# Two of four row tiles turned by TensorE, new plan costs for DMA turns, and seven block products for eight at the end of a fused quantised layer

## The chip, the cores and the metric

The kernel runs on one core of one Trainium2 chip, as one launch. The metric is the device time of that launch in microseconds (us). The profiler also gives one profiled execution, with a span from its first to its last instruction. A smaller time is better.

TensorE (PE) multiplies into PSUM, VectorE (DVE), ScalarE (ACT) and GpSimd (POOL) work elementwise, and SyncE (SP) issues most transfers. A DMA turn is a transfer that transposes 128-row blocks on its way within SBUF.

## What is computed

`x` is two batches of 1024 rows by 2048, `ctx` two matrices of 2048 x 2048, `weight` one matrix of 2048 x 2048, all f32.

```python
def fake_quant(x, scale, zp):
    q = jnp.clip(jnp.round(x / s + z), 0, 255)
    return (q - z) * s

# first product
x = x + tanh(g_xattn) * (fake_quant(layernorm(x)) @ fake_quant(ctx))
# second product: rows to int8 by their own largest value, weights to -1, 0, 1
h = layernorm(x)
s = 127 / clip(max(abs(h), axis=-1), 1e-5)
xq = clip(round(h * s), -128, 127) / s
scale_w = 1 / clip(mean(abs(weight)), 1e-5)
tw = clip(round(weight * scale_w), -1, 1)
x = x + tanh(g_ffn) * (einsum('bsi,oi->bso', xq, tw) / scale_w)
```

Each second product is therefore 1024 x 2048 x 2048 per batch, with rows that are whole numbers and weights that are -1, 0 or 1.

## The kernel before

**Tiles.** The rows are 16 tiles of 128; tiles 0 to 7 are batch 0, tiles 8 to 15 batch 1. In each batch they are taken in the order 6, 7, 0, 1, 2, 3, 4, 5 (`last_first`, L970; `rows` for batch 1, L1052). A tile's rows stay in `resid` as f32 from load (L351) to store (L829).

**First product.** `norm1` (L371) takes a tile's statistics (L378), quantises it to int16 on ScalarE (L434) and clips it to f16 on VectorE (L437). The tile is then turned, so that its columns lie on partitions: in batch 0 by PE with 128x128 transposes into PSUM (L444) and two evictions (L450), in batch 1 by one DMA turn on SP's queue (L454). Row sums come from GpSimd additions in batch 0 (L460 to L465) and from ScalarE in batch 1 (L473). `context` (L526) loads blocks of the context (L541), quantises them on ScalarE (L547), clips them on VectorE (L550) and adds them for a column term (L557, `column_term` L574). All of them come to rest in `ca`, in two halves h of 1024 columns. `first(t, h)` (L602) is 16 steps of two f16 matmuls with 512 columns (L611), and an addition to the rows (L620). `terms` (L635) adds the row and column terms (L640).

**Second product.** `norm2` (L660) takes one or two tiles: squares with their sum on ScalarE (L677), largest value on VectorE (L684), small operations on one number per row (L690 to L709). `norm2_tile` (L736) quantises to int16 on ScalarE (L748), casts to f16 on VectorE (L757) and turns the tile: by PE (L762) with two evictions (L768), of which the first `by_act` go to ScalarE and the rest to VectorE, or by a DMA turn (L774). `second(t, h, ...)` (L801) is 16 matmuls for each 512 columns: 8 pairs of blocks, f16 rows stationary, fp8 weights moving (L814), then an addition with the row's scale (L823) and a store (L829), by SP for two tiles of batch 1 and by GpSimd for all others.

**Weights.** They are loaded twice in part (L854), summed (L865), quantised (L899), clipped to fp8 (L903) and turned in units of two bytes: output blocks 0 to 5 by PE (L909, L913), 6 to 15 by DMA turns (L917). They rest in `tw`, four units q of 512 columns. Until then `tw` and `ca` also serve as landing places.

**What sets the order.** Nothing is issued where it stands in the code. Each `step(engine, weight, due, do, rd, wr, take, give, dma, hold, port)` only books a piece of work: its engine, its planned time, a due time, its keys read and written, and a buffer that it takes from a pool (`work`: 4, `tp` for turned rows: 5, `mm`: 3 PSUM tiles, `tr`: 2). `dma` is the planned time of a transfer on the shared DMA engines, and `port` marks work that VectorE and GpSimd may only do one at a time in the plan. `Plan.order` (L62) simulates the engines with these costs, always issuing the step that can begin first, and of several the one that is due first. `Plan.latest` (L123) works new due times back from the end. `give_out` (L153) does both ten times, keeps the shortest plan and issues its steps in that order. So a changed cost of one step may move instructions on any engine.

For a DMA turn, the plan has the queue's own share as the weight and the transfer as `dma`, and SP is held in the plan until earlier transfers are through (L108 and L109):

```python
if dma:
    if port is None:
        end = free[engine] = max(end, dma_free)
    dma_free = max(dma_free, end) + dma
```

**Stages.** Batch 0's first products with h=0, then with h=1, with `norm2` of tiles 6 and 7 as soon as these are done, then of 0 and 1 (L975). The second product of tiles 6, 7, 0 and 1 goes unit by unit along with the arrival of the turned weights (L1005 to L1021), with 128-column matmuls for unit 0. Then tiles 2 to 5. In batch 1 (L1067 to L1092) tiles are planned in pairs, and the planner is free to place second products of the first tiles before first products of the last ones.

Of the kernel before, what the change touches and what calls it, by code (L numbers as in the profile page):

```python
# [9 lines left out]
F32 = mybir.dt.float32  # L10
# [13 lines left out]
class Plan:  # L24
# [128 lines left out]
    def give_out(self):  # L153
        steps = self.steps
        waits = [len(s[4]) for s in steps]
        follow = [[] for _ in steps]
        for n, s in enumerate(steps):
            for m in s[4]:
                follow[m].append(n)
        due, best = [s[2] for s in steps], None  # L160
        for i in range(self.ROUNDS):
            order, ends, passed = self.order(due, follow, waits)
            if best is None or max(ends) < best[0]:
                best = (max(ends), order)
            due = self.latest(ends, passed, follow)
        for n, slot in best[1]:
            if slot is None:
                steps[n][3]()
            else:
                steps[n][3](slot)  # L170
# [3 lines left out]
def flamingo_gated_kernel(  # L174
# [117 lines left out]
    plan = Plan({"work": NWORK, "tp": NTP, "mm": 3, "tr": 2})  # L292
    step = plan.step
    aT, qT, pm = {}, {}, {}
    taken = {}

    def scalars():

        s = {}

        def spread(slot):
            s["pp"] = tr[slot]
            nc.tensor.matmul(s["pp"][:, 2:6], ones32[0:1, :], par1[:, 2:6], start=True, stop=True)
            nc.tensor.matmul(s["pp"][:, 0:2], ones32[0:1, :], tg1, start=True, stop=True)

        def of(i, rs, zc):
            nc.vector.reciprocal(rs, par[:, i : i + 1])  # L310
            nc.vector.tensor_scalar(zc, par[:, i + 1 : i + 2], CENTER, None, ALU.subtract)

        def rest():
            nc.vector.scalar_tensor_tensor(g1, par[:, 2:3], par[:, 4:5], tg[:, 0:1], ALU.mult, ALU.mult)
            nc.vector.scalar_tensor_tensor(g1d1, zc1, -1.0, g1, ALU.mult, ALU.mult)
            nc.vector.scalar_tensor_tensor(g1d2, zc2, -1.0, g1, ALU.mult, ALU.mult)
            nc.vector.tensor_scalar(kd2, zc2, -float(K), None, ALU.mult)
            nc.vector.tensor_scalar(gkd, kd2, g1d1, None, ALU.mult)

        step("ACT", 0.3, 0.0, lambda: nc.scalar.activation(tg1, par1[:, 0:2], AF.Tanh), wr=[("tg1",)], hold=4.0)  # L320
        by = step("PE", 0.6, 6.0, spread, rd=[("tg1",)], wr=[("pp",)], take="tr", hold=6.8)
        step(
            "DVE", 0.2, 6.0, lambda: nc.vector.tensor_copy(par, s["pp"][:, 0:6]), rd=[("pp",)],
            wr=[("par",)], give=[by],
        )
        step("DVE", 0.3, 6.1, lambda: of(2, rs1, zc1), rd=[("par",)], wr=[("p1",)])
        step("DVE", 0.3, 6.2, lambda: of(4, rs2, zc2), rd=[("par",)], wr=[("p2",)])
        step("DVE", 0.9, 10.0, rest, rd=[("p1",), ("p2",)], wr=[("g",)])

    def res(t):  # L330
        return resid[:, t % MT, :]

    def xk(t, h=None):
        return [("x", t % MT, i) for i in ((0, 1) if h is None else (h,))]

    strip = const.tile([P, 30 * 2 * MT], F32, name="strip")
    stats6 = const.tile([P, 4, K // 512, nc.vector.BN_STATS_DIM], F32, name="stats6")
    used = [0]

    def tiny(n=1):  # L340
        used[0] += n
        return strip[:, used[0] - n : used[0]]


    def load_x(t, due, queue, halves=1, hold=0.0):
        w = K // halves
        for h in range(halves):

            def bring(h=h):
                q = nc.sync if queue == "SP" else nc.gpsimd  # L350
                q.dma_start(out=res(t)[:, ts(h, w)], in_=xrow[t][:, ts(h, w)])  # L351

            keys = xk(t) if halves == 1 else xk(t, h)
            step(queue, 0.5, due, bring, wr=keys, dma=2.55 / halves, hold=hold)

    def newton(v, sd):

        n = v.shape[1]
        r, f = tiny(n), tiny(n)
        nc.vector.reciprocal(r, sd)  # L360
        if n == 1:
            nc.vector.tensor_scalar(f, v, r, r, ALU.mult, ALU.mult)
            nc.vector.tensor_scalar(f, f, -0.5, 1.5, ALU.mult, ALU.add)
            nc.vector.tensor_scalar(r, r, f, None, ALU.mult)
        else:
            nc.vector.scalar_tensor_tensor(f, r, -0.5, r, ALU.mult, ALU.mult)
            nc.vector.tensor_mul(f, f, v)
            nc.vector.scalar_tensor_tensor(r, f, 1.5, r, ALU.add, ALU.mult)
        return r

    def norm1(group, dues, by_pe, fold_it, place=None, pieces=1, on_dve=False):  # L371

        n = len(group)
        s = {"mv": tiny(2 * n)}
        key = lambda *a: ("n1", group[0]) + a

        def stats(t, c):
            nc.vector.bn_stats(stats6[:, t % 4, c, :], res(t)[:, ts(c, 512)])  # L378

        def aggr(j, t):  # L380
            nc.vector.bn_aggr(s["mv"][:, ts(j, 2)], stats6[:, t % 4].rearrange("p c s -> p (c s)"))

        def root():
            s["sd"] = tiny(n)
            nc.scalar.activation(s["sd"], s["ve"], AF.Sqrt)

        def var():
            mv = s["mv"].rearrange("p (n s) -> p s n", s=2)
            s["mean"], s["ve"] = mv[:, 0, :], tiny(n)
            nc.vector.tensor_scalar(s["ve"], mv[:, 1, :], LN_EPS, None, ALU.add)  # L390

        def scale():
            r = newton(s["ve"], s["sd"])
            sc, bi = s["sc"], s["bi"] = tiny(n), tiny(n)
            nc.vector.tensor_scalar(sc, r, rs1, None, ALU.mult)
            if n == 1:
                nc.vector.tensor_scalar(bi, s["mean"], sc, -1.0, ALU.mult, ALU.mult)
            else:
                nc.vector.scalar_tensor_tensor(bi, s["mean"], -1.0, sc, ALU.mult, ALU.mult)
            nc.vector.tensor_scalar(bi, bi, zc1, None, ALU.add)  # L400

        for j, t in enumerate(group):
            for c in range(4):
                step(
                    "DVE", 0.69, dues[j], (lambda t, c: lambda: stats(t, c))(t, c), rd=xk(t, c // 2),
                    wr=[("st", t % 4)],
                )
            step(
                "DVE", 0.3, dues[j], (lambda j, t: lambda: aggr(j, t))(j, t), rd=[("st", t % 4)],
                wr=[key("mv")],  # L410
            )
        due = dues[-1]
        step("DVE", 0.16, due, var, rd=[key("mv")], wr=[key("ve")])
        step("ACT", 0.2, due, root, rd=[key("ve")], wr=[key("sd")])
# [4 lines left out]

    def norm1_tile(t, due, by_pe, fold_it, place, pieces, ready, scales, on_dve):  # L420

        s = {}
        key = lambda *a: ("n1t", t) + a
        n = K // pieces

# [699 lines left out]
```

## Time and profile before

| what | us |
|---|---|
| runs, median of 3 | 498.71 (497.04, 498.71, 499.32) |
| profiled execution, its own time | 496.74 |
| its span | 495.0 |
| PE busy | 467.6 |
| VectorE busy | 340.6 |
| ScalarE busy | 276.6 |
| GpSimd busy | 63.5 |
| mean granted clock of TensorE | 0.995 |

1.74 us of the profiled execution lie outside its span. Five groups of instructions, by line and shape, with count, busy time and mean:

| group | count | busy us | mean ns |
|---|---|---|---|
| L611 matmuls 128x512, f16 | 1024 | 230.8 | 379 to 384 |
| L814 matmuls 128x512, fp8 weights | 976 | 214.8 | 379 to 381 |
| L814 matmuls 128x128, fp8 weights | 192 | 11.5 | 219 |
| L762 transposes 128x128 (rows of the second product) | 32 | 2.3 | 219 |
| L774 DMA turns of such rows | 14 | - | - |

The mean time of a matmul is from its start to the end of its own passage; matmuls overlap, so start to start they are closer. The profile names engines as above; "PEld" is PE's load of stationary data, "SPq" SP's queue. A row of 40 digits shows the span in 40 slices of 12.4 us, each digit being the busy share in tenths; the row "PEclk" is the clock that TensorE was granted. In a list of waits, the columns are the total of the waits, their number and the longest. In a timeline, the columns are start, length, engine, line and operation, with the idle time ahead and what ended it in brackets.

### The profile page before, as it was taken

To read this page: it belongs to the slowest core of one execution; us is meant where nothing else is said; L and a number is where in the kernel's file an instruction comes from. 1 tells how busy PE (TensorE), PEld (TensorE's weight loads), DVE (VectorE), ACT (ScalarE), POOL (GpSimd) and SP (SyncE) were. 2 spreads that over 40 slices of the span, in tenths; PEclk is the share of its full clock that TensorE was granted. 3 is DMA by queue.
4 is the path that set the end of the run, shared out by engine and by line. 5 is a ranking of instruction groups with operands and counts; after the bars stand their busy time and mean duration, and the time that the engine had idled before them with its cause. 6 is when DMAs were issued, how large, how long until landed. Compare 5 with 4: busy or idle time off the path is not lost.

```text
span 495.0 us, 6179 instructions
## 1 busy us (share of the span) xinstructions
PE 467.6 (94%) x2422; PEld 223.0 (45%) x2422; DVE 340.6 (69%) x568; ACT 276.6 (56%) x258; POOL 63.5 (13%) x76
## 2 busy tenths in 40 slices
PE   0599999999998799999999999999999999999996
PEld 0244454444467344444444444444444444444442
DVE  4999989959999688556697957632989831572122
ACT  4997896878999988631488364530454430050000
POOL 0574529100000020100100100000000000000000
PEclk9999999999999899999999999999999999999999
DMA  8999968992189999999999995610041542215122
GB/s 293 425 419 424 366 214 338 428 407 81 60 215 366 260 301 295 306 258 330 402 363 341 297 269 189 100 28 1 0 66 47 144 111 102 86 61 153 79 92 85
DMA packets 76170, 108.94 MB, mean 220 GB/s; under 512 B 58220, under 2 KB 58220, under 8 KB 70892
## 3 DMA queue, kind: packets, MB, share of 16 engines
q1 hardware_dynamic: 72064, 93.86, 60.1%
q0 software_dynamic: 4064, 14.68, 7.7%
q8 instruction: 19, 0.31, 0.2%
q14 instruction: 11, 0.09, 0.1%
q10 hardware_dynamic: 12, 0.00, 0.0%
HBM read 77.59 MB, written 16.78 MB: 191 GB/s over the span
## 4 chain that ended last, share of the span: by engine, by line
PE 76%; DVE 14%; DMA 6%; issue 2%; ACT 1%; DVEq 0%
PE mm L814 40%; PE mm L611 32%; DVE resid L640 3%; DMA resid<-in_x_dram 2%; PE tr L814 2%; DVE strip L684 2%; DMA tw<-in_ctx_dram 2%; DVE resid L620 2%; DMA tw<-ca 2%; DVE stats L378 1%; DVE ca L550 1%; DVE ca L903 1%; ACT ca L547 1%; PE tr L444 1%; DVE colg L557 1%
## 5 line engine op out<-in xcount | busy, mean ns | idle before, releaser
L814 PE MATMUL mm<-tw,turned 128*128 128x512 fp8e4 (+1 forms) x1104 | 211.9, 353 | 4.7 <-DMA turned<-work 2.4
L611 PE MATMUL mm<-ca,turned 128*128 128x512 f16 x832 | 187.7, 384 | 0.5 <-DVE ca L550 0.3
L814 PEld LDWEIGHTS <-turned 128*128 128x128 f16 x1168 | 106.8, 98 | 122.7 <-issue 6.3
L611 PEld LDWEIGHTS <-turned 128*128 128x128 f16 x832 | 81.8, 99 | 99.0 <-issue 4.8
L823 DVE SCALAR_TENSOR_TENSOR resid<-mm,am,resid 128x1024 f32<-128x1024 f32 (+1 forms) x31 | 38.6, 1246 | 64.3 <-PE mm L814 64.2
L547 ACT ACTIVATE ca<-ca,scal 128x2048 int16<-128x2048 f32 (+1 forms) x30 | 50.5, 1692 | 36.9 <-DMA ca<-in_ctx_dram 36.4
L677 ACT ACTIVATE work<-resid,strip 128x1024 f32<-128x1024 f32 x32 | 36.4, 1138 | 57.8 <-DVE strip L668 54.1
L829 POOL DMA_DIRECT2D out_dram<-resid x30 | 18.1, 606 | 362.5 <-DVE resid L823 225.2
L620 DVE SCALAR_TENSOR_TENSOR resid<-mm,scal,resid 128x1024 f32<-128x1024 f32 x32 | 40.4, 1277 | 18.4 <-PE mm L611 18.2
L378 DVE BATCH_NORM_STATS2 stats<-resid 128x6 f32<-128x512 f32 x64 | 40.0, 678 | 7.9 <-DMA resid<-in_x_dram 7.9
L550 DVE TENSOR_SCALAR ca<-ca 128x2048 f16<-128x2048 int16 (+1 forms) x40 | 27.3, 698 | 24.5 <-ACT ca L547 24.5
L611 PE MATMUL mm<-ca,tw 128*128 128x512 f16 x192 | 43.1, 379 | 0.4 <-DVE tw L450 0.2
L748 ACT ACTIVATE work<-resid,strip 128x2048 int16<-128x2048 f32 x16 | 35.5, 2263 | 12.2 <-DVE strip L704 7.8
L684 DVE TENSOR_REDUCE strip<-work 128x1 f32<-128x1024 f32 x32 | 37.3, 1210 | 1.3 <-ACT work L677 1.3
L640 DVE SCALAR_TENSOR_TENSOR resid<-colg,rowg,resid 128x2048 f32<-128x2048 f32 x16 | 37.4, 2344 | 0.1
L434 ACT ACTIVATE work<-resid,strip 128x2048 int16<-128x2048 f32 (+1 forms) x17 | 33.4, 1984 | 1.3 <-DVE strip L400 1.3
L557 DVE TENSOR_TENSOR colg<-colg,ca 128x2048 f16<-128x2048 f16 x24 | 30.8, 1304 | 0.3
L611 PEld LDWEIGHTS <-tw 128*128 128x128 f16 x192 | 18.4, 98 | 22.8 <-DVE tw L450 0.7
L899 ACT ACTIVATE work<-ca,scal 128x2048 int16<-128x2048 f32 x13 | 25.6, 2005 | 1.6 <-DMA ca<-in_L_ffn_weight_dram 1.1
L473 ACT ACTIVATE work<-work,scal 128x2048 f16<-128x2048 f16 x8 | 16.0, 1994 | 18.5 <-DMA turned<-work 18.5
L865 ACT ACTIVATE tw<-ca 128x2048 int8<-128x2048 f32 x10 | 19.1, 1910 | 7.6 <-DMA ca<-in_L_ffn_weight_dram 7.5
L462 POOL TENSOR_TENSOR tw<-tw,work 128x512 f16<-128x512 f16 x16 | 21.8, 1364 | 1.6 <-DVE work L437 0.4
(93 smaller groups left out, 260.7 us busy)
## 6 DMA issues: line engine op xcount, KB each, us to landing
ca<-in_L_ffn_weight_dram SPq DMA_DIRECT2D x19, 1024.0 KB, 8.6
ca<-in_ctx_dram SPq DMA_DIRECT2D x16, 1024.0 KB, 12.3
resid<-in_x_dram SPq DMA_DIRECT2D x15, 1024.0 KB, 11.7
out_dram<-resid POOLq DMA_DIRECT2D x26, 512.0 KB, 3.8
tw<-in_ctx_dram SPq DMA_DIRECT2D x8, 1024.0 KB, 12.6
ca<-in_ctx_dram SPq DMA_DIRECT2D x14, 512.0 KB, 8.4
tw<-in_L_ffn_weight_dram SPq DMA_DIRECT2D x6, 1024.0 KB, 6.8
out_dram<-resid SPq DMA_DIRECT2D x3, 512.0 KB, 2.6
```

What stands on the lines that cost most here:

```text
L378: nc.vector.bn_stats(stats6[:, t % 4, c, :], res(t)[:, ts(c, 512)])
L434: nc.scalar.activation(d, v, AF.Identity, bias=bi, scale=sc)
L547: nc.scalar.activation(a.bitcast(I16), s["w"], AF.Identity, bias=zc2, scale=rs2)
L557: nc.vector.tensor_add(r, r, a2(kt - kt % 2, h * H, 2 * H))
L611: nc.tensor.matmul(pm[t][:, ts(q, U)], aT[t][:, kt, :], a2(kt, h * H + q * U, U), start=(kt == 0), stop=(kt == KT - 1),)
L620: nc.vector.scalar_tensor_tensor(v, pm[t], g1, v, ALU.mult, ALU.add)
L640: nc.vector.scalar_tensor_tensor(v, colg, rowg[:, t : t + 1], v, ALU.add, ALU.add, accum_out=acc[:, i : i + 1])
L677: nc.scalar.activation(s["dev", t, h], res(t)[:, ts(h, H)], AF.Square, bias=s["nm"][:, j : j + 1], accum_out=s["s2"][:, k : k + 1],)
L684: nc.vector.tensor_reduce(s["m2"][:, k : k + 1], s["dev", t, h], AX.X, ALU.max)
L748: nc.scalar.activation(s["q"].bitcast(I16).rearrange("p (k j c) -> p k j c", j=2, c=P), v.rearrange("p (k c j) -> p k j c", j=2, c=P), AF. ...
L814: nc.tensor.matmul(pm[t][:, o + b0 * P : o + b1 * P], qT[t][:, k, j, :], w8[:, k, j, b0 * P : b1 * P], start=(k + j == 0), stop=(k + j == PB),
L823: nc.vector.scalar_tensor_tensor(v, pm[t][:, 0 : n * U], am[:, t : t + 1], v, ALU.mult, ALU.add)
```

## The change

1. **Two plans.** `give_out` is split: `rounds(kept)` runs the ten rounds and keeps the given due times of the first steps, `give_out(order)` issues. The kernel's planning becomes `build(SEVEN)`. It is planned once with `SEVEN=0`, and the due times of the steps up to batch 1's products are kept for the plan that is issued, with `SEVEN=2`.
2. **DMA turns in the plan.** A turn of rows is booked as 4.5 of SP and 0.8 of the DMA engines (before 1.3 and 3.8), a turn of weights as 2.4 and 0.6 (before 1.3 and 1.9).
3. **Tiles 6 and 7** of the second product are turned by PE, like 0 and 1, and all four have one eviction on ScalarE and one on VectorE.
4. **Batch 1.** All first products come ahead of all second ones in the code. `norm2` takes one tile at a time, with forms of the small operations that take one number per row as a scalar. The cast of L757 goes to ScalarE.
5. **Seven products for eight.** For the last two pairs of row tiles (tiles 10, 11 and 12, 13), the two tiles of a pair, split in halves of the inner dimension, and the weights, split in halves both ways, are taken as 2 x 2 blocks. `seven` forms four sums of row blocks on VectorE (f16, 128x1024), `weight_differences` four differences of weight blocks on GpSimd (fp8, 64 pieces of 128x512), stored in the half of `ca` that held the context with h=0. Seven block products of 2 x 8 matmuls then take the place of eight; some are summed up in PSUM and added to the rows in between (`take`). The very last is done and stored in two parts of 512 columns.

The core of the diff, leading blanks left out:

```diff
@@ Plan
-    def give_out(self):
+    def rounds(self, kept=()):
...
-        due, best = [s[2] for s in steps], None
+        due, best = list(kept) + [s[2] for s in steps[len(kept) :]], None
...
-            due = self.latest(ends, passed, follow)
+            due = list(kept) + self.latest(ends, passed, follow)[len(kept) :]
+        return best[1:]
@@ turn_dma of norm1_tile; that of norm2_tile is booked alike
-                "SP", 1.3, due, turn_dma, rd=q_keys, ..., take="tp",
-                dma=3.8, port=None,
+                "SP", 4.5, due, turn_dma, rd=q_keys, ..., take="tp",
+                dma=0.8, port=None,
@@ terms
-            wr=xk(t) + [("acc", i)],
+            wr=xk(t) + [("acc", i)], port=SEVEN > 0 and t >= MT,
@@ norm2
+            def var_alone():
+                vm = s["vm"] = tiny(2)
+                s2, m2, ve, big, least = s["s2"], s["m2"], vm[:, 0:1], vm[:, 1:2], tiny()
+                nc.vector.tensor_scalar(ve, s2[:, 0:1], s2[:, 1:2], None, ALU.add)
+                nc.vector.tensor_scalar(ve, ve, 1.0 / N, LN_EPS, ALU.mult, ALU.add)
...
@@ norm2_tile
+            def cast_act():
+                nc.scalar.copy(s["q"], s["q"].bitcast(I16))
...
+            if SEVEN and t >= MT:
+                step("ACT", 2.1, due, cast_act, wr=[key("q")])
+            else:
         step("DVE", 0.69, due, cast, wr=[key("q")], port=True)
@@ weight_quant
-                "SP", 1.3, due, turn_dma, ..., dma=1.9, port=None,
+                "SP", 2.4, due, turn_dma, ..., dma=0.6, port=None,
@@ batch 0
-            norm2([t - 1, t], [due - 6.9, due], n == 3, by_act=2)
+                norm2([t - 1, t], [due - 6.9, due], True, by_act=1)
@@ new
+        def weight_differences(dues, engines):
+            for i, (due, by) in enumerate(zip(dues, engines)):
+                for q in range(2):
+                    b11, b12, b21, b22 = w_part(q, 0), w_part(q + 2, 0), w_part(q, 1), w_part(q + 2, 1)
+                    pair = ((b12, b11), (b22, t_part(0, q)), (b22, b12), (b21, t_part(1, q)))[i]
...
+                    w = HK * 2 * U // PIECES[by]
+                    for c in range(PIECES[by]):
+                        def go(i=i, q=q, by=by, pair=pair, at=ts(c, w)):
+                            eng = nc.vector if by == "DVE" else nc.gpsimd
+                            eng.tensor_tensor(
+                                t_part(i, q)[:, at], pair[0][:, at], pair[1][:, at], ALU.subtract, saturate=False
+                            )
...
+        PIECES = {"DVE": 4, "POOL": 8}
+        ENGINES = ("POOL",) * 4
+        def seven(pair, i, due, last):
...
+            def sums(n):
+                if n == 0:
+                    nc.vector.tensor_add(s1, flat[u][:, 0:half], a22())
+                elif n == 1:
+                    nc.vector.tensor_sub(s2, s1, a11())
+                elif n == 2:
+                    nc.vector.tensor_sub(flat[u][:, 0:half], a11(), flat[u][:, 0:half])
+                else:
+                    nc.vector.tensor_sub(s4, a12(), s2)
...
+            product("y", a11, lambda q: w_part(q, 0), ..., due, start=True)
+            take("y", t, 0, due + d)
+            product("x", a12, lambda q: w_part(q, 1), ..., due + d, start=True)
+            store(t, 0, take("x", t, 0, due + 2 * d, give=True), due + 2 * d)
+            product("y", lambda: s2, lambda q: t_part(1, q), ..., due + 2 * d)
+            take("y", t, 1, due + 3 * d)
+            product("z", lambda: s1, lambda q: t_part(0, q), ..., due + 3 * d, start=True)
+            take("z", u, 1, due + 4 * d)
+            product("y", lambda: flat[u][:, 0:half], lambda q: t_part(2, q), ..., due + 4 * d)
+            store(u, 1, take("y", u, 1, due + 5 * d), due + 5 * d)
+            product("z", lambda: s4, lambda q: w_part(q + 2, 1), ..., due + 5 * d)
+            store(t, 1, take("z", t, 1, due + 6 * d, give=True), due + 6 * d)
+            for q in range(2):
+                product("y", a22, lambda q: t_part(3, q), ..., due + 6 * d, qs=(q,), give=give)
+                if last:
+                    store(u, 0, take("y", u, 0, due + 7 * d, q == 1, q), due + 7 * d, q)
...
@@ batch 1
-    order += [(t, h) for t in rows[4:] for h in range(2)]
+        order += [(t, h) for t in rows[4:6] for h in range(2)]
+        order += [(t, h) for h in range(2) for t in rows[6:]]
...
-        if n in (5, 7):
-            norm2(rows[n - 5 : n - 3], [due - 16.0, due - 8.0], False)
+            if n == 5:
+                alone(rows[:2], due)
+            if n == 7:
+                alone(rows[2:4], due)
+        weight_differences([due + 20.0, due + 30.0, due + 40.0, due + 50.0], ENGINES)
...
+            if n >= MT - 2 * SEVEN:
+                seven(pair, n // 2 - MT // 2 + SEVEN, due, n == MT - 2)
+                due += 7 * UNIT
...
-    plan.give_out()
+    plan, before = build(0)
+    due = plan.rounds()[0][:before]
+    plan, _ = build(2)
+    plan.give_out(plan.rounds(due)[1])
```

## The prediction

> **What bounds the kernel now.** I read the page first: busy shares, the 40 slices, the chain.
>
> ```profile
> PE 467.6 (94%) x2422; PEld 223.0 (45%) x2422; DVE 340.6 (69%) x568; ACT 276.6 (56%) x258; POOL 63.5 (13%) x76
> ...
> PE   0599999999998799999999999999999999999996
> ...
> PEclk9999999999999899999999999999999999999999
> DMA  8999968992189999999999995610041542215122
> ...
> PE 76%; DVE 14%; DMA 6%; issue 2%; ACT 1%; DVEq 0%
> ```
>
> PE is full except at the start, at the very end, and in two slices from 148.5 to 173 us, where its clock dips too. TensorE work sets the time, so only three things count: PE work, PE waits, the tail. The waits of PE are few:
>
> ```profile
> PE tr L444 <- DVE work L437: 9.4, 3, 7.3
> PE tr L306 <- DMA par<-in_L_xattn_x_zp_dram: 6.9, 1, 6.9
> PE mm L814 <- DMA turned<-work: 2.4, 1, 2.4
> PE mm L814 <- DMA tw<-ca: 2.3, 1, 2.3
> PE tr L814 <- ACT turned L768: 1.1, 1, 1.1
> ```
>
> The first two are the start, which the change leaves alone. The other three stand together in PE's timeline, where the second product begins:
>
> ```profile
> 153.60 2.85 PE L814 MATMUL mm<-tw,turned 128*128 128x128 fp8e4 x48 [2.35 <-DMA turned<-work]
> ...
> 163.36 3.61 PE L814 MATMUL tr<-tw,turned 128*128 128x512 fp8e4 x16 [1.10 <-ACT turned L768]
> ...
> 169.31 12.21 PE L814 MATMUL mm<-tw,turned 128*128 128x512 fp8e4 x48 [2.33 <-DMA tw<-ca]
> ```
>
> In windows of 2.5 us, 167.5 to 175 was granted 0.88, 0.50, 0.94, which loses 0.3 + 1.25 + 0.15 = 1.7 us. Waits plus clock: 5.8 + 1.7 = **7.5 us lost**. SP's queue shows where the first wait comes from: the DMA turns of tiles 6 and 7 hold SP, and five weight reloads stand behind them.
>
> ```profile
> 138.09 5.26 SPq L774 DMA_TRANSPOSE turned<-work  x1
> ...
> 144.11 5.88 SPq L774 DMA_TRANSPOSE turned<-work  x1
> 150.10 3.80 SPq L854 DMA_DIRECT2D ca<-in_L_ffn_weight_dram  x5
> ```
>
> **Seven products for eight.** Of the second product's 512-wide matmuls, two pairs of row tiles need 224 in place of 256. One piece of the chain is 160 of them in 34.53 us, 0.216 us each: −32 x 0.216 = **−6.9 us**, at the very end, where nothing but PE is late.
>
> **Turning tiles 6 and 7 by PE.** +32 transposes 128x128. Eight of the same kind take 0.45 us from start to start (132.16 to 132.61): 4 x 0.45 = **+1.8 us**. Four more evictions go to VectorE, 4 x 0.68 = 2.7 us, in a stretch where VectorE and ScalarE are full (9.76 and 10.00 of 10 us in 140 to 150). ScalarE stays at four, since the pair that PE turned already now shares its evictions with VectorE. Gone are two DMA turns, 5.26 + 5.88 = 11.1 us of SP, and PE's wait of 2.35 on them. The five reloads behind can then land by about 152; I put their old landing at about 165 (estimate: start 150.1, 1 MB each at about 2.6 us, sharing with turns from 158.7). The weight turns still wait for weight quantisation on the two full engines (first at 158.74 before; about 160.5 after, by adding up the built queues, those 2.7 us included), but no longer share the DMA with the reloads. I put the loss here at 3.8 us in place of 7.5 (range 2 to 6): one wait for weights stays.
>
> **The order behind it.** The planner now books a row turn as 4.5 us of SP and 0.8 of DMA (1.3 and 3.8 before), and batch 1 makes all first products ahead of all second ones. So PE meets the second half of batch 1's context with 7.7 us less work behind it. In the trace its last block was ready at 312.9 and PE asked for it at 313.9: 1.0 us of slack.
>
> ```profile
> 308.35 0.42 DVE L550 TENSOR_SCALAR ca<-ca 128x1024 f16<-128x1024 int16 x1
> ...
> 312.48 0.43 DVE L550 TENSOR_SCALAR ca<-ca 128x1024 f16<-128x1024 int16 x1 [0.44 <-ACT ca L547]
> ```
>
> After, PE asks at 313.9 − 7.7 = 306.2 with the old loss, at 302.5 with 3.8 lost. DMA is full from 140 to 300 (the slices), so the block moves only as far as the transfers do: about 7 us of weight-turn time freed by the early reloads, less 1.8 us later start, 5.2 us; and 1.6 us more because no row quantisation (L434) stands between the last context quantisations on ScalarE. Ready at about 306. PE then waits about 3.4 us: what was saved at 150 is **given back at 306**. Loss in all: 3.8 + 3.4 = 7.2.
>
> **Tail.** After, both 512-wide adds of the last block wait for the last matmul, where before the first one lay beside PE; they share a PSUM tile. One more add: 0.75 us, **+0.7**.
>
> ```profile
> 487.17 1.28 DVE L823 SCALAR_TENSOR_TENSOR resid<-mm,am,resid 128x1024 f32<-128x1024 f32 x1 [2.70 <-PE mm L814]
> 490.63 0.75 DVE L823 SCALAR_TENSOR_TENSOR resid<-mm,am,resid 128x512 f32<-128x512 f32 x1 [2.17 <-PE mm L814]
> ```
>
> **At nothing.** Casts of batch 1 on ScalarE (8 x about 2.0, like L473's 1.99), single-tile norms (about 3 us more of small VectorE work), sums on VectorE (8 x about 0.7): behind 310 us the slices show VectorE and ScalarE with free time, and each row tile is ready some 10 us ahead. Without that cover a late row costs what it is late, and a late sum at most its 0.7.
>
> **Differences of the weights on GpSimd.** 64 subtractions 128x512 in fp8. They may start when the last first product with h=0 frees the context's first half (PE's work adds up to 353), and the 61st is needed at 452.5, the last at 455.9: 99.5 us for 61, with 9 stores x 0.6 = 5.4 us between them. The trace has no fp8 there; the nearest row is f16:
>
> ```profile
> L462 POOL TENSOR_TENSOR tw<-tw,work x16: 1151/1160/2022, 16.8 to 83.8; 128x512 f16<-128x512 f16 x16
> ```
>
> By its mean of 1.364, plus 0.08 between two: 61 x 1.444 + 5.4 = 93.5 us. The Trainium skill (SBUF — State Buffer, "Who interferes with whom") says that a GpSimd operation and a VectorE one with two SBUF inputs exclude each other for whole instructions. By that rule I take the undisturbed 1.155 + 0.08, 61 x 1.235 = 75.3, and add every such VectorE operation of the window: five L640 x 2.34 = 11.7 and four sums, 2.8, and the stores: 95.2. Both are under 99.5, so I take nothing; but the slack is 4 to 6 us. The same skill (GPSIMD Engine Reference, "Engine selection") puts elementwise work of two inputs on VectorE, GpSimd being about 2x slower: it speaks against placing 64 there, yet the trace's own 1.16 already holds that. Bounds for fp8: 1.0 (half the bytes; still no gain, since nobody waits) to 2.0, where 61 x 2.08 + 19.9 = 147 is 47 us late. I stay with 1.16: the row has the same element count.
>
> **Sum.** −6.9 + 1.8 + 0.7 + (7.2 − 7.5) = **−4.7 us**. Against the profiled execution's 496.74 (span 495.0) this gives 492.0; that execution lies 2.0 under the median of the runs, 498.71, so the forecast is 498.71 − 4.7 = **494.0**.
>
> **Rivals.** *Full gain.* The context isn't late, because the new order of SP's queue serves it first: loss 3.8, change −8.1, 490.6. For it: two row turns fewer ahead of it. Against: 1.0 us of slack before, full DMA.
>
> *Context no earlier.* The block stays ready at 312.9 (its quantisation or its loads bound by something else): PE's loss is 14.2 in all and the gain is eaten: +2.3, 501.0. Break-even is a context 2.2 us earlier.
>
> *Differences late (slower).* One mechanism: GpSimd, at PE's products from 452.5 on. From 1.305 a piece start to start, undisturbed, PE waits; each 0.1 more is 6 us; at 1.38 the gain of 4.7 is gone. At 1.48 (fp8 a fifth dearer than f16): 90.3 + 19.9 = 110.2, 10.7 late, 498.71 − 4.7 + 10.7 = 504.7. For it: no row has fp8, the spread up to 2022 ns. Against: the median at 1160.
>
> **Chances.** Main case 0.42 (own range 492 to 496.5), full gain 0.18, context no earlier 0.18, differences late 0.17, a new wait for VectorE's evictions at 150 of 2 to 5 us 0.05. A measurement here tells about 0.5%, 2.5 us, from no change. Faster: 0.42 + 0.18 = 0.60; same: 0.18 and part of the last, 0.21; slower 0.19. Range 489 to 502: it leaves out most of the late differences and the tip of the full gain.
>
> **What would show it.** PE's waits on turned rows at 150 gone, one on tw left, the clock there full or dipped once; a wait on L550 near 300 to 306 of 2 to 5 us (full gain: none; no earlier: 7 or more); GpSimd's subtractions at 1.1 to 1.4 us, ended before PE's first use; 720 + 224 matmuls of 512; two adds of 0.75 at the end. Wrong if PE waits for "ca" from GpSimd after 440, or if the context's wait is of another size.

## The result and the profile after

| | before | after |
|---|---|---|
| runs, median of 4 | 498.04 (497.04 to 499.32) | 519.30 (517.82 to 520.31) |
| span of the profiled execution | 495.0 | 516.6 |

The change makes the kernel slower by 21.3 us: ratio 1.0423, with a 95% interval from 1.0384 to 1.0462. The forecast was 494.0, with a range from 489 to 502. (Executions of one kernel below can differ by up to 4%; a ratio compares executions with the kernel before run beside them and leaves out those of either kernel that took over 1.5% more than its shortest.)

A "row turn" is a DMA turn of a row tile, a "weight turn" one of weights; a "hole" is a stretch in which PE loses time; the "hold" of a DMA instruction is the time for which it keeps SP's queue. First the page of the changed kernel, to set beside the rows shown before:

```profile
PE 467.4 (90%) x2422; PEld 222.3 (43%) x2422; DVE 386.0 (75%) x666; ACT 292.8 (57%) x270; POOL 136.9 (27%) x140
...
PE   0699999999998999299994899999999999977995
...
PEclk9999999999999999699997999999999999998999
DMA  8999879980497999999999982310013222252123
```

The dip at 150 to 173 is nearly gone, and three new ones are there, in slices of 12.9 us: at 207, at 271 and at 452 to 478. The same digits in PE's waits:

```profile
PE mm L861 <- DMA turned<-work: 9.2, 1, 9.2
...
PE mm L861 <- DVE resid L870: 6.1, 1, 6.1
PE mm L981 <- DVE resid L1004: 3.1, 1, 3.1
PE mm L625 <- DVE resid L870: 3.0, 2, 1.9
PE mm L981 <- DVE ca L961: 2.7, 1, 2.7
PE tr L861 <- DVE turned L811: 1.2, 1, 1.2
```

L861 is the second product (L814 before), L625 the first (L611), L870 its addition (L823), L981 a block product of the seven, L1004 its addition, L961 a sum.

To see where time goes, I added up, over windows of 2.5 us, the idle time of PE and the part of its busy time that the granted clock withheld. "Span less loss" is what remains. "E" rows are the experiments below, one traced execution each.

| lost by PE, us, between | 0-140 | 140-190 | 190-235 | 235-310 | 310-440 | 440-485 | to the end | span less loss |
|---|---|---|---|---|---|---|---|---|
| before | 17.2 | 7.3 | 0 | 0 | 0 | 0 | 4.4 | 466.1 |
| after | 17.4 | 1.3 | 11.3 | 11.0 | 0 | 8.6 | 5.3 | 461.6 |
| E1 old costs | 20.3 | 4.0 | 0 | 2.5 | 3.0 | 8.5 | 5.3 | 458.9 |
| E2 new costs alone | 24.7 | 8.0 | 9.1 | 11.4 | 0.2 | 0 | 4.4 | 463.4 |
| E4 no differences | 21.2 | 2.1 | 14.5 | 8.7 | 0 | 0 | 5.2 | 458.0 |
| E8 old costs, no differences | 19.7 | 3.9 | 0 | 10.9 | 0 | 0 | 5.3 | 457.8 |
| E11 old costs of rows | 19.1 | 2.2 | 6.1 | 0 | 0 | 7.2 | 5.3 | 460.0 |
| E12 old costs of weights | 20.4 | 6.7 | 0 | 22.0 | 7.4 | 6.0 | 5.6 | 460.5 |
| E16 old costs of rows, copies | 21.3 | 3.4 | 5.6 | 0 | 0 | 0 | 5.3 | 458.9 |

After against before: 26.1 us more lost, 4.5 us less work, 21.6 in all, which is the difference of the spans. The new holes are 11.3, 11.0 and 8.6, 30.9 in all; 6.0 is won back at 140 to 190. The first column differs between executions by some us even where nothing was changed ahead of 140 (17.4 after, 21.2 in E4), and so does the last (461.6 after, 458.0 in E4, whose PE work is the same).

**At 205 to 222**, in SP's queue of the changed kernel (start, length of the hold, line):

```profile
192.59 1.58 SPq L555 DMA_DIRECT2D ca<-in_ctx_dram  x3
194.28 21.80 SPq L818 DMA_TRANSPOSE turned<-work  x2
216.18 1.21 SPq L555 DMA_DIRECT2D ca<-in_ctx_dram  x2
```

and of the kernel before:

```profile
196.30 1.78 SPq L774 DMA_TRANSPOSE turned<-work  x1
198.13 1.64 SPq L541 DMA_DIRECT2D ca<-in_ctx_dram  x3
202.27 14.95 SPq L774 DMA_TRANSPOSE turned<-work  x2
```

The same turn, issued 2 us earlier but behind three loads, holds SP 15.2 us instead of 1.78 (the first of the two in 21.80). PE asked for it at 208.4 and went on at 217.6, when it had landed.

**At 264 to 305** the page names VectorE's addition, which is not what was late. A mixed timeline of the changed kernel:

```profile
263.32 0.43 DVE L564 TENSOR_SCALAR ca<-ca 128x1024 f16<-128x1024 int16 x1 [4.70 <-ACT ca L561]
...
271.98 1.24 ACT L561 ACTIVATE ca<-ca,scal 128x1024 int16<-128x1024 f32 x1 [1.14 <-DMA ca<-in_ctx_dram]
...
273.25 0.43 DVE L564 TENSOR_SCALAR ca<-ca 128x1024 f16<-128x1024 int16 x1 [1.10 <-ACT ca L561]
...
276.37 0.43 DVE L564 TENSOR_SCALAR ca<-ca 128x1024 f16<-128x1024 int16 x1 [0.44 <-ACT ca L561]
276.83 1.23 DVE L571 TENSOR_TENSOR colg<-colg,ca 128x2048 f16<-128x2048 f16 x1
277.97 1.28 DVE L870 SCALAR_TENSOR_TENSOR resid<-mm,am,resid 128x1024 f32<-128x1024 f32 x1
279.30 3.04 PE L861 MATMUL mm<-tw,turned 128*128 128x512 fp8e4 x7 [6.08 <-DVE resid L870]
```

The addition at 277.97 takes a product that PE had ended by 268.5. It stands in VectorE's queue behind clips of context blocks (L564) and of a row tile (L451, not shown), which wait for ScalarE. What ScalarE waited for in 235 to 310:

```profile
ACT work L487 <- DMA turned<-work: 17.3, 4, 8.5
...
ACT ca L561 <- DMA ca<-in_ctx_dram: 4.9, 5, 2.3
```

L487 is a row tile's sum, which overwrites the rows that the tile's DMA turn reads, and so has to wait for that turn. So it was row turns more than loads of context. Only the addition frees the PSUM tile that PE wants: a late turn or load reaches PE through ScalarE's and VectorE's queues, well before PE needs the tile or block itself (after 140 PE never waits for L564).

**At 452 to 480**, VectorE and GpSimd:

```profile
456.46 5.97 DVE L959 TENSOR_TENSOR ca<-turned 128x1024 f16<-128x1024 f16 x1
...
466.05 9.34 DVE L965 TENSOR_TENSOR ca<-turned,ca 128x1024 f16<-128x1024 f16 x1
```

```profile
456.57 5.30 POOL L937 TENSOR_TENSOR ca<-tw,ca 128x512 fp8e4<-128x512 fp8e4 x5
...
466.39 8.45 POOL L937 TENSOR_TENSOR ca<-tw,ca 128x512 fp8e4<-128x512 fp8e4 x8
```

A sum takes 0.68 us alone. L959 ends at 462.43, which is 0.56 after the end of GpSimd's run of five (461.87); L965 ends at 475.39, 0.55 after the run of eight (474.84). VectorE waited not for one subtraction but for the whole run. L654 (the terms, 2.34 us alone) took 8.99 in the same way at 417. But it isn't always so: at 402 another L654 got in after less than one subtraction, in the middle of a run of nine.

```profile
402.41 3.00 DVE L654 SCALAR_TENSOR_TENSOR resid<-colg,rowg,resid 128x2048 f32<-128x2048 f32 x1
```

```profile
399.00 11.57 POOL L937 TENSOR_TENSOR ca<-tw,ca 128x512 fp8e4<-128x512 fp8e4 x9
```

### The profile page after: what moved, and what is told of

The parts are those of the page before. It is cut to its first block, busy times and chain, and to the rows that moved or that the text cites. A ratio compares the mean times of both kernels' runs of the same rounds, so it can differ in the third digit from the quotient of the medians.

```text
span 516.6 us, 6378 instructions
## 1 busy us (share of the span) xinstructions
PE 467.4 (90%) x2422; PEld 222.3 (43%) x2422; DVE 386.0 (75%) x666; ACT 292.8 (57%) x270; POOL 136.9 (27%) x140
## 4 chain that ended last, share of the span: by engine, by line
PE 61%; DVE 15%; DMA 13%; SPq 6%; ACT 2%; issue 2%; DVEq 0%; ACTq 0%
PE mm L625 39%; PE mm L861 12%; PE mm L981 7%; DMA ca<-in_ctx_dram 6%; DMA turned<-work 5%; DVE resid L654 4%; SPq L468 3%; SPq L1122 2%; DVE resid L870 2%; DVE ca L965 2%; DVE strip L698 2%; DMA colg<-in_L_ffn_weight_dram 1%; DVE ca L959 1%; PE tr L458 1%; ACT ca L561 1%
## 5 line engine op out<-in xcount | busy, mean ns | idle before, releaser
L625 PE MATMUL mm<-ca,turned 128*128 128x512 f16 x832 | 187.3, 384 | 4.2 <-DVE resid L870 3.0
L861 PE MATMUL mm<-tw,turned 128*128 128x512 fp8e4 (+1 forms) x848 | 157.6, 347 | 15.9 <-DMA turned<-work 9.2
L861 PEld LDWEIGHTS <-turned 128*128 128x128 f16 x912 | 81.7, 99 | 105.5 <-issue 10.6
L625 PEld LDWEIGHTS <-turned 128*128 128x128 f16 x832 | 81.7, 99 | 103.6 <-issue 8.4
L876 POOL DMA_DIRECT2D out_dram<-resid x26 | 16.1, 621 | 218.7 <-DVE resid L870 100.7
L561 ACT ACTIVATE ca<-ca,scal 128x2048 int16<-128x2048 f32 (+1 forms) x30 | 50.4, 1690 | 26.5 <-DMA ca<-in_ctx_dram 26.5
L937 POOL TENSOR_TENSOR ca<-tw 128x512 fp8e4<-128x512 fp8e4 x32 | 39.3, 1253 | 79.8 <-PE mm L625 79.8
L691 ACT ACTIVATE work<-resid,strip 128x1024 f32<-128x1024 f32 x32 | 36.4, 1139 | 21.6 <-DVE strip L682 21.2
L564 DVE TENSOR_SCALAR ca<-ca 128x2048 f16<-128x2048 int16 (+1 forms) x40 | 27.1, 683 | 27.9 <-ACT ca L561 27.9
L654 DVE SCALAR_TENSOR_TENSOR resid<-colg,rowg,resid 128x2048 f32<-128x2048 f32 x16 | 45.9, 2867 | 0.1
L625 PE MATMUL mm<-ca,tw 128*128 128x512 f16 x192 | 43.1, 379 | 0.0
L487 ACT ACTIVATE work<-work,scal 128x2048 f16<-128x2048 f16 x8 | 16.0, 2002 | 43.6 <-DMA turned<-work 43.6
L937 POOL TENSOR_TENSOR ca<-tw,ca 128x512 fp8e4<-128x512 fp8e4 x32 | 36.1, 1155 | 0.0
L1004 DVE SCALAR_TENSOR_TENSOR resid<-mm,am,resid 128x1024 f32<-128x1024 f32 (+1 forms) x15 | 18.0, 1209 | 19.6 <-PE mm L981 19.6
L870 DVE SCALAR_TENSOR_TENSOR resid<-mm,am,resid 128x1024 f32<-128x1024 f32 x22 | 28.1, 1278 | 5.6 <-PE mm L861 5.6
L571 DVE TENSOR_TENSOR colg<-colg,ca 128x2048 f16<-128x2048 f16 x24 | 29.5, 1256 | 0.2
L625 PEld LDWEIGHTS <-tw 128*128 128x128 f16 x192 | 18.6, 98 | 21.5
## 6 DMA issues: line engine op xcount, KB each, us to landing
out_dram<-resid POOLq DMA_DIRECT2D x26, 512.0 KB, 4.7
ca<-in_ctx_dram SPq DMA_DIRECT2D x14, 512.0 KB, 7.1
out_dram<-resid SPq DMA_DIRECT2D x3, 512.0 KB, 2.6
```

The costliest lines, as they stand in the source:

```text
L561: nc.scalar.activation(a.bitcast(I16), s["w"], AF.Identity, bias=zc2, scale=rs2)
L625: nc.tensor.matmul(pm[t][:, ts(q, U)], aT[t][:, kt, :], a2(kt, h * H + q * U, U), start=(kt == 0), stop=(kt == KT - 1),)
L654: nc.vector.scalar_tensor_tensor(v, colg, rowg[:, t : t + 1], v, ALU.add, ALU.add, accum_out=acc[:, i : i + 1])
L691: nc.scalar.activation(s["dev", t, h], res(t)[:, ts(h, H)], AF.Square, bias=s["nm"][:, j : j + 1], accum_out=s["s2"][:, k : k + 1],)
L861: nc.tensor.matmul(pm[t][:, o + b0 * P : o + b1 * P], qT[t][:, k, j, :], w8[:, k, j, b0 * P : b1 * P], start=(k + j == 0), stop=(k + j == PB),
L870: nc.vector.scalar_tensor_tensor(v, pm[t][:, 0 : n * U], am[:, t : t + 1], v, ALU.mult, ALU.add)
```

## The experiments

The theory after the traces: (a) the new plan costs of the DMA turns put turns right behind loads, which makes the first two holes; (b) VectorE's operations with two SBUF inputs wait for runs of GpSimd (the plan books both on one `port`, hence "port theory"), which makes the third. Rivals: batch 1's new order asks for the context too early, whatever the turns cost; VectorE is late from its own load. Diffs are against the kernel named; "old costs" are 1.3 and 3.8 for rows, 1.3 and 1.9 for weights.

**E1, old costs in the changed kernel.**

```diff
-                    "SP", 4.5, due, turn_dma, ... dma=0.8, port=None,
+                    "SP", 1.3, due, turn_dma, ... dma=3.8, port=None,
-                    "SP", 2.4, due, turn_dma, ... dma=0.6, port=None,
+                    "SP", 1.3, due, turn_dma, ... dma=1.9, port=None,
```

> The changed kernel with the plan costs of the DMA turns as before (1.3 of SP and 3.8 of DMA for rows, 1.3 and 1.9 for weights). Queue theory (the new plan costs put turns behind context loads, and loads behind turns): the two holes of PE at 205 to 222 (10.8 us) and 264 to 305 (11.0 us) mostly go: 519 less 15 to 22, 498 to 504. Rival (the holes come from batch 1's new order, which asks for the context earlier, whatever the turns cost): 514 to 520.

The median is 513.97, a gain of 5 us and at the edge of the rival's forecast. The profiled execution took 504.3, the others 512.0 to 517.5. In the profile (table) 11.3 and 11.0 became 0 and 2.5, while the third hole stayed (3.0 and 8.5). So with the old costs both holes can go; what the three longer executions lost, no trace shows, and E1 alone does not decide.

**E2, the new costs in the kernel before**, the same edit the other way round.

> The kernel before with only the new plan costs of the DMA turns. Queue theory: PE waits for turned rows or for context between 190 and 310, 508 to 518. Rival (batch 1's order): no difference, 495 to 501.

519.69, ratio 1.0452 (1.0406 to 1.0497). The costs alone, with nothing else of the change, bring 22 us, and the holes stand at the same places: 9.1 and 11.4 (and 7.5 more before 140, where executions differ anyway). The new order of batch 1 isn't needed for the holes; that it makes none of its own at 235 to 310 is seen in E11 and E16, which have it and lose nothing there.

**E3, one turn moved ahead of the three loads**, nothing planned anew.

```diff
-    plan.give_out(plan.rounds(due)[1])
+    order = plan.rounds(due)[1]
+    turn = next(i for i, (n, _) in enumerate(order) if n == 602)
+    loads = [e for e in order[:turn] if e[0] in (682, 659, 662)]
+    order = [e for e in order[: turn + 1] if e not in loads] + loads + order[turn + 1 :]
+    plan.give_out(order)
```

> The changed kernel with one thing moved: the DMA turn of the first row tile after the four (issued at 194) goes ahead of the three context loads issued just before it. Queue theory: the hole at 205 to 222 shrinks from 10.8 us to 3 or less, part of it may come back at 264 to 305 since those loads are some 2 to 4 us later: 509 to 516. Rival (the turn is late because the transfers are full, in whatever order): hole stays, 518 to 521.

517.95, ratio 1.0404 (1.033 to 1.0478): no gain that can be told, and 13.7 us lost at 190 to 235. Its SP queue:

```profile
195.76 1.64 SPq L818 DMA_TRANSPOSE turned<-work  x1
197.46 1.66 SPq L555 DMA_DIRECT2D ca<-in_ctx_dram  x3
201.90 12.71 SPq L818 DMA_TRANSPOSE turned<-work  x1
```

The moved turn now holds 1.64 us, as the theory says. But the next turn stands behind the loads instead, and PE waits 6.9 us for that one at 216. That a turn waits for the loads ahead of it held for the turn that was moved; but the hole did not shrink to 3 us or less, and the time is about where the rival had it.

**E4, differences planned but not issued** (the block products use old contents).

```diff
                         def go(i=i, q=q, by=by, pair=pair, at=ts(c, w)):
+                            return
                             eng = nc.vector if by == "DVE" else nc.gpsimd
```

> The changed kernel with the weight differences on GpSimd left out (planned, but not issued; the block products then use old contents). Port theory (VectorE's operations with two SBUF inputs wait for whole runs of GpSimd subtractions): the hole of 8.5 us at 455 to 480 goes, L654's longest falls from 8989 ns to about 2345, 510 to 512. Rival (VectorE is late there because of the single-tile norms' small operations): 517 to 520.

510.84, ratio 1.0282 (1.0245 to 1.0318): 8.5 us faster, with the loss at 440 to 485 gone and L654 back at its old mean:

```profile
L654 DVE SCALAR_TENSOR_TENSOR resid<-colg,rowg,resid 128x2048 f32<-128x2048 f32 x16 | 37.5, 2345 | 0.1
```

The single-tile norms run in this kernel as well, so by themselves they are not the cause.

**E5, only the turning of tiles 6 and 7 by PE**, in the kernel before.

```diff
-            norm2([t - 1, t], [due - 6.9, due], n == 3, by_act=2)
+            norm2([t - 1, t], [due - 6.9, due], True, by_act=1)
```

> The kernel before with tiles 6 and 7 turned by PE and nothing else (plan costs as before). If the saving at 150 to 173 (7.4 us lost before, about 2 after) is kept: 498 less 5.5 plus 1.8, 493 to 496. If PE, arriving earlier, only meets turned rows or the context later on, it is given back: 498 to 502, with a wait between 200 and 310.

496.43, ratio 0.9978 (0.9957 to 0.9999): 1.1 us, between the two theories. Lost at 140 to 190: 3.9, where 7.3 was lost before; of these 3.4 us, 1.8 should go to the transposes by the prediction's sum, and 0.7 came back at 313.

**E6, two turns ahead of all but one of four loads.**

```diff
+    for loads, turn in (((682, 659, 662, 670), 602), ((659, 662, 670), 605)):
+        held = [e for e in order if e[0] in loads]
+        order = [e for e in order if e[0] not in loads]
+        i = next(i for i, (n, _) in enumerate(order) if n == turn) + 1
+        order[i:i] = held
```

> The changed kernel with only SP's order altered: the first two row turns at 194 go ahead of all but one of the context loads that stood before them (four loads moved behind). Queue theory (a turn takes as long as the loads ahead of it in the transfers): the hole at 205 to 228 goes (2 us or less), the context is later by some 3 to 8 us and part of the gain returns at 265 to 305: 507 to 516. Rival (transfers are simply full): a hole of 8 or more stays before 230.

516.36, ratio 1.0399 (1.0354 to 1.0444). The loss at 190 to 235 fell from 11.3 to 5.2, and that at 235 to 310 rose from 11.0 to 15.1. (That execution took 520.11, the longest of four.) The first hole became smaller, not 2 us or less as forecast, and the rest moved on.

**E7, old costs, and GpSimd made to wait where the plan has VectorE on the port:** a copy of one column on GpSimd behind L654 of batch 1 and behind each sum.

```diff
                 nc.vector.scalar_tensor_tensor(
                     v, colg, rowg[:, t : t + 1], v, ALU.add, ALU.add, accum_out=acc[:, i : i + 1]
                 )
+                if SEVEN and t >= MT:
+                    nc.gpsimd.tensor_copy(gate, acc[:, i : i + 1])
...
+                nc.gpsimd.tensor_copy(gate, (s1, s2, flat[u], s4)[n][:, 0:1])
```

> The changed kernel with the old plan costs of the turns, and with one tiny copy on GpSimd behind each VectorE operation of batch 1 that the plan books on the shared port (five of L654 and the eight sums): GpSimd waits there, so that VectorE gets the port where the plan says. Port theory: no VectorE operation takes more than about 3 us, the 10 us of holes after 390 go: 491 to 497, and runs agree within 1%. Rival (the late holes come from VectorE's load as such, or GpSimd is now late itself): 500 or more.

Median of 19 runs 496.92 (488.27 to 507.44), ratio 0.9925 (0.9887 to 0.9963), for which 8 of the 19 count. In the profile (span 488.0) no L654 takes longer than 2.351 us, the sums take 0.68 to 0.96, and PE waits for nothing after 166:

```profile
L656 DVE SCALAR_TENSOR_TENSOR resid<-colg,rowg,resid x16: 2341/2344/2351, 112.4 to 416.1; 128x2048 f32<-128x2048 f32 x16
```

The port theory holds; that runs agree within 1% does not. By its ratio this is the best of the kernels here that compute everything; by the median of all its runs it is level with E5 (496.43) and E16 (496.76).

**E8, old costs and no differences** (E1's edit with E4's).

> The changed kernel with the old plan costs, the weight differences on GpSimd left out (planned but not issued, old contents used). Port and queue theory together: both causes gone, 491 to 495, runs within 1%. If something else in batch 1 is slow: 498 or more.

Median 493.92 (488.56 to 504.26), ratio 0.9837 (0.9806 to 0.9867), which is 490 and for which 8 of 16 count; that runs agree within 1% failed here too. The profiled execution took 499.37, with a wait of PE of 9.3 us on a row turn at 275. SP's queue has the same order as in E1, yet the two turns before that wait hold SP longer. E1, then E8:

```profile
264.82 12.92 SPq L468 DMA_TRANSPOSE turned<-work  x2
```

```profile
263.50 19.53 SPq L468 DMA_TRANSPOSE turned<-work  x2
```

In E7, with that order too, they hold it for 11.27. So one order of SP's instructions can give the late turn or not.

**E9, E7's copies with the new costs.**

> The changed kernel with the new plan costs and with the tiny copies on GpSimd behind VectorE's operations on the shared port. Port theory: the hole at 455 to 480 goes as it did without the differences, no VectorE operation with two SBUF inputs over about 3.5 us, 509 to 513. Rival (taking the differences away helped only because GpSimd's work itself was in the way): 516 to 520.

512.10, ratio 1.0268 (1.0211 to 1.0325), as without the differences (1.0282). Nothing is lost at 440 to 485 although all 64 subtractions are there, so GpSimd's work as such is not in the way. (One L656 still took 4.86 us, over the 3.5 forecast, and cost nothing.) Since E3's trace lost nothing there without any copies, this trace alone would not settle it; E16 against E11 does.

**E10, old costs, eight products, no differences.**

```diff
-        weight_differences([due + 20.0, due + 30.0, due + 40.0, due + 50.0], ENGINES)
...
-            if n >= MT - 2 * SEVEN:
+            if n >= MT:
```

> The changed kernel with the old plan costs, eight block products instead of seven for the last two pairs, and no differences: what is left is tiles 6 and 7 by PE and batch 1's new order. The seven products' term of the sum (6.9 less 0.7 for the tail): 6 us over the undisturbed 490 of the kernel with seven and without differences, 494 to 498. If seven products give nothing on net: 489 to 492.

497.68, ratio 0.9989 (0.9963 to 1.0015). Against E8's 0.9837, seven products give 1.5%, 7.6 us, if the differences cost nothing. In the traces the span less loss agrees: 465.4 in E10, 457.8 in E8.

**E11 and E12, old costs for the row turns alone, and for the weight turns alone.**

> The changed kernel with the old plan costs for row turns alone. If the row turns' costs make the holes at 205 and 265: the time of both costs old, 504 to 512. If those of the weight turns do (loads set between weight turns at 178): 516 to 521.

> The changed kernel with the old plan costs for weight turns alone. If the row turns' costs make the holes: 514 to 521. If the weight turns' do: 504 to 512.

E11: 503.56, ratio 1.0112 (1.0069 to 1.0156); lost 6.1, 0 and 7.2 at 190, 235 and 440. E12: 528.34, ratio 1.0585 (1.0528 to 1.0642), with a wait of 18.5 us on a row turn near 275. Most of the time lost goes with the costs of the row turns: 1.0423 became 1.0112 without them, 15.5 us of 21.3. The second hole goes with them (0 in E11, 22.0 in E12). The first does not go with them alone: with old costs of rows and new ones of weights 6.1 remains, and in E12 it is missing. But there PE reaches 190 some 8.4 us later than after (20.4 and 6.7 lost until then, against 17.4 and 1.3), so this is no measure of the weights' share.

**E13 and E14: how?** By adding up what the transfers moved in windows of 10 us, from 200 to 290 the kernel before moved 29.4 MB, the changed one 26.2, E1 29.3 and E2 26.5. E13 moves three turns back so that turns stand in pairs; E14 gives the second half of batch 1's context to GpSimd's queue.

```diff
+    for turn, mate in ((621, 624), (770, 774), (793, 797)):
+        i = next(i for i, (n, _) in enumerate(order) if n == turn)
+        moved = order.pop(i)
+        i = next(i for i, (n, _) in enumerate(order) if n == mate)
+        order.insert(i, moved)
```

```diff
-                q = nc.sync if queue == "SP" else nc.gpsimd
+                q = nc.sync if queue == "SP" and (b, h) != (1, 1) else nc.gpsimd
```

> The changed kernel with three of SP's row turns moved back behind loads so that turns stand in pairs (turn, loads, turn becomes loads, turn, turn), three times between 217 and 290. If a turn between loads costs the transfers their rate (from 200 to 290 the changed kernel moved 26.2 MB where the one before moved 29.4): more MB by 290, the hole at 265 to 305 falls from 11 us to 6 or less: 511 to 516. If only the order of what is needed first matters: moved turns are later, hole as large or larger: 518 to 525.

> The changed kernel with the 16 context loads of batch 1's second half issued by GpSimd instead of SP, in the same planned order: SP's turns no longer hold them. If it is SP's hold that makes the context late: the hole at 265 to 305 falls to 5 or less, 510 to 515. If it is the rate of the transfers themselves: hole stays, 517 to 523 (also if the loads now stand behind GpSimd's stores).

E13: 522.55, ratio 1.0468 (1.0388 to 1.0549), 25.0 MB in its profile. E14: 520.51, ratio 1.042 (1.0347 to 1.0493), with three turns holding SP 30.2 us in its profile. Neither helps, which speaks against the switching and against SP's hold on the loads. (The profiles are of the longest of four executions each, 528.87 and 531.67, and the sizes in them say little.)

**E15, loads and turns kept apart in time:** ahead of a row turn SP reads one column of the last load's landing place.

```diff
+    def after_load():
+        if last[0] is not None:
+            nc.sync.dma_start(out=gate, in_=last[0])
+            last[0] = None
...
+                after_load()
                 nc.sync.dma_start_transpose(aT[t], s["q"])
```

> The changed kernel where SP, ahead of each row turn behind a load of batch 1, first reads 4 bytes per row of that load's landing place, so that the turn starts only when the load has landed (or been worked on). If a turn is slow because loads are in flight beside it: a row turn holds SP 1.6 to 4 us in place of 5 to 15, and the eight turns from 190 to 290 hold it under 35 us in all, against 70; the time may fall (505 to 515) or not, since waiting costs too. If turns are slow for another reason: holds as before, 520 or more.

526.61, ratio 1.0568 (1.049 to 1.0645). A part of its SP queue:

```profile
195.12 1.56 SPq L566 DMA_DIRECT2D ca<-in_ctx_dram  x3
210.99 0.54 SPq L307 DMA_DIRECT2D gate<-ca  x1
211.63 4.12 SPq L832 DMA_TRANSPOSE turned<-work  x2
215.85 1.36 SPq L566 DMA_DIRECT2D ca<-in_ctx_dram  x2
225.68 0.48 SPq L307 DMA_DIRECT2D gate<-ca  x1
226.26 1.64 SPq L832 DMA_TRANSPOSE turned<-work  x1
```

Between 190 and 300 eight turns hold SP 13.9 us in all, against 70.2 in the changed kernel: a turn with no load ahead of it takes 1.6 to 2.1 us, however it is planned. But SP now waits 70.7 us for the landings themselves, as long as the turns had held it. So the hold looks to be the wait for the loads ahead, and the kernel is no faster for moving it.

**E16, old costs for rows, new ones for weights, with E7's copies.**

> The changed kernel with the old plan costs for row turns alone and with the tiny copies on GpSimd. Both causes together: 503.6 less the late hole of 6.6 us in that kernel's profile, 494 to 498, and no wait of PE after 440. If the late hole is not the port's: 501 or more.

496.76, ratio 0.9977 (0.9951 to 1.0002), nothing lost from 235 to 485. Against E11 the copies alone make 6.7 us by the ratios, about the 7.2 that E11 lost at 440 to 485: all 64 subtractions still run, and only who waits for whom has changed. The two causes add up, and with the new weight costs a hole of 5.6 us stays at 190 to 235.

## Why the prediction was wrong

Two steps failed. The prediction gave the new plan costs no term of their own: for 140 to 310 it had 7.2 us lost in all, and 23.6 were lost (1.3, 11.3 and 11.0). And it put VectorE's sums next to GpSimd's subtractions at nothing, where 8.6 us were lost. Point by point:

- **Bound, and PE's work.** Right. −5.1 was forecast for matmuls and transposes, and 466.1 became 461.6, −4.5, as near as this can be told (kernels with the same PE work show 457.6 to 462.2). Seven products were sized at −6.9 + 0.7 for the tail; E8 against E10 has −7.6.
- **150 to 173.** Right in kind. With the turning alone (E5) 3.9 us is lost there, where I said 3.8; after, it is 1.3. (My 7.5 for before is 7.3 by the table: I had counted a lowered clock in a window in which PE was mostly idle.)
- **"Ready at about 306 ... given back at 306", 3.4 us.** This is the first step that failed. I took the transfers' rate as given and moved the last context block by what was freed ahead of it. The last clip of a context block came at 318.5, and PE had lost 22.3 us from 190 on by then, none of it on the block itself: 11.3 at 205 on a turned row, for which the prediction has no term at all (its "each row tile is ready some 10 us ahead" is said of the time behind 310), and 11.0 at 264 to 305 through ScalarE's and VectorE's queues. The cause is the edit that I named in a sentence and priced at nothing of its own, the new plan costs (E2: 22 us alone; E11: 15.5 us for those of the rows). The rows of before held the warning: one turn held SP 1.78 us at 196.30, and the next two, behind three loads, 14.95.
- **"Context no earlier"**, the rival for this, had the right resource, but priced it as one late block (+2.3), not as a slower supply of turns and context over 90 us.
- **"Differences late".** GpSimd was not late: a piece took 1.09 us (1.16 taken), and PE never waited for it. The second failing step is the one under "at nothing", that a late sum costs "at most its 0.7", and in the sum by the port's rule, that GpSimd pays for the overlap. VectorE paid: 5.97 and 9.34 us for sums of 0.68, 8.5 us of PE (E4; 6.7 in E16 against E11). The Trainium skill (SBUF — State Buffer, "Who interferes with whom") says that whoever issues first keeps the pair for the whole instruction. E3 fits that: L965 took 1.58 us, its own 0.68 and the rest of one subtraction. The changed kernel goes beyond it: there the sums got in only after runs of five and eight subtractions, so that the price was the run and not the instruction.
- **Tail.** 0.9 more, 0.7 forecast.

With both causes taken out, the rest of the sum comes out near the forecast: −4.7 us is a ratio of 0.9906, and E7 has 0.9925, though only over the 8 of its 19 executions that the ratio counts.

What remains open is how the costs of the row turns make turns and context late. Their holds look like waits for the loads ahead (1.64 against 15.2 us for the same turn in E3; E15), but neither pairs (E13), nor another queue (E14), nor keeping them apart (E15: 24.6 MB from 200 to 290) brought the 3 MB back that are missing there. Nor is the order of SP's instructions enough to explain it: with one order E1 moved 29.3 MB, E7 29.6 and E8, with its late turn, 26.0. Fewer bytes may as well be a consequence of the late turns as their cause. Also open is when VectorE gets in between GpSimd's subtractions and when not.

## What to carry to other kernels

A cost in a planner is an edit of the whole order: build it, and price each queue by what stands directly ahead of each step that is needed soon, with rows from the trace for both the lone and the crowded case. When work is given to an idle engine, ask not only whether that engine is in time, but whom it keeps waiting, and for how long a run. Where a plan says that two engines take turns on something, nothing makes them do it unless one waits for the other: a copy of one column was enough.

## What the runs showed of the hardware that I had not expected

- A DMA turn of a 128x2048 f16 tile holds its queue 1.6 to 1.8 us with no load ahead of it and up to 15.2 us behind three 1 MB loads.
- A VectorE operation with two SBUF inputs waited for 5 and 8 GpSimd subtractions in a row (5.97 and 9.34 us). In E3, with the same instructions in that stretch, the two engines alternated instead (L959 1.86 us, L965 1.58 at most), and the loss there was 0: the outcome is not fixed by the order of instructions. Nor by who starts first in the records: in both, L959 starts 0.11 us ahead of GpSimd's run of five.
- With one order of SP's instructions, two DMA turns near 264 held the queue 11.27 (E7), 12.92 (E1) or 19.53 us (E8).
- A wait of 9.2 us of PE cost about 10.7: the clock was at 0.50 when it resumed (217.5 to 220) and 0.87 on the mean of the next 2.5 us.
